# One transformer block for 16 sequences: the feed-forward's chain moved one gap on, its input transposed by VectorE in 32 by 32 blocks, and the head reordered

## The chip, the cores and the metric

The kernel runs on one core of a Trainium2 chip. The metric is the time of one execution on the device in microseconds; of the kernel before there are three timed runs, 646.89, 648.42 and 648.76, and one execution under the profiler, from which every duration below comes.

The engines are called PE (matrix products; its weight loads have a row of their own, PEld), DVE or VectorE, ACT or ScalarE, POOL or GpSimd, and SP (which here only issues transfers). Each works through its own queue in order.

## The reference

Sixteen sequences of 256 tokens with 256 features go through one block, all in float32:

```python
x = x + attention(layernorm(x), wq, wk, wv, wo)    # 16 heads of 16; key j is masked for query i if j - i > 16
x = x + feed_forward(layernorm(x))                 # down(silu(gate(x)) * up(x)), 1024 wide
```

The three weights of the feed-forward are not given as matrices. Each is a cubic spline through 2033 control points, sampled at 262,144 places, and has to be built on the chip.

## The kernel before

**Steps.** The loop over `s` (line 788) runs 20 steps; in the steady part one step works on several sequences at once. `nb = s - 1` has the maxima of its scores found, `tb = s - 2` has its exponentials and values computed, `ob = s - 3` gets its attention output projected and its second norm, sequence `s - 4` goes through the feed-forward, and `pb = s + 3` has q, k and v projected. Scores are computed twice: once for the row maxima (`find_max`, VectorE, tile `z`), once with the maximum as a seventeenth row of k and q for the exponentials (`e`, ScalarE, then a causal cut on POOL).

**Gaps.** PE's four score groups of a step (`inner` 0 and 1, `outer` 0, `inner` 2 and 3, `outer` 1) use the same two PSUM tiles, `scores0` and `scores1`. So a group can only start when VectorE and ScalarE have read the one before it. Between the groups lie numbered gaps, and the order of the work in them is written out by hand: `project(s, gap)` (line 761, with the table `early` for steps 0 to 3, line 721) and `fill(s, gap)` (line 692), which deals out the feed-forward:

- `gate_up(b, i)` (line 588), i = 0 to 3: a quarter of gate and of up (tiles `pg`, `pu`), then tanh on ScalarE (`th`) and two products on VectorE (`th`, `inter`). With `columns=32` each product is issued as four of 32 columns.
- `down(b, c)` (line 609), c = 0 and 1: one half of the tokens, 8 products of PE (`pd`), one add on VectorE into `x`; after c = 1 the sequence's output is sent by SP. Before, `down` could be split again into halves.

Before the change gate_up 0 of a sequence stands in gap 7 of the step in which its second norm is made; gate_up 1, 2 and 3 and down 0 and 1 follow in gaps 1, 3, 4, 5 and 6 of the next step. For steps from 13 on, where nothing is left to project, they stand in gaps 1, 2, 3, and the four half downs in 4, 5, 6 and 6.5.

**The second norm.** In gap 5 `project_o` (line 555, PE tile `py`, needs `divide`) and `stats_f` run, then `norm_f` (line 572, VectorE, tile `xnf`). In gap 6 `turn_f` (line 575) transposes `xnf` into `x2T`, which gate and up read: four PE transposes by the identity into the PSUM tile `ptf`, then a copy by ScalarE.

**The softmax's chain.** `turn_max` (line 486) transposes the maxima (`pm`), copies them (`mxT`) and has SP send them into `qk` in four transfers; the next step's second scores read them. `gather` sends the sums and outputs (`den`, `ac`), `invert` makes reciprocals (`rec`), sends them out and back spread (`rd`, `rb`), and `divide` multiplies before `project_o`. All of it goes through SP's queue.

**The head.** Steps 0 to 3 also load the input, normalise and transpose the first sequences with PE (`stats_a`, `norm_a`, `turn_a`: `xna`, `pta`, `xT`), fill the constant rows of `qk` and `v` with POOL memsets (`scores_and_values`), and build the weights (`spline` through `part`: products `pw`, a ScalarE copy, a predicated VectorE copy). With the home "ssss" the spline's products lie in the two score tiles. `spread(b)` sends q and k of a sequence to `qk` in eight SP transfers.

Nearly every instruction is recorded under line 88, that of the helper that keeps the order; so the profile's groups are told apart by tiles.

Of the kernel before, what the change touches and what calls it, by code (L numbers as in the profile page):

```python
# [11 lines left out]
F32 = mybir.dt.float32  # L12
BF16 = mybir.dt.bfloat16
AF = mybir.ActivationFunctionType
ALU = mybir.AluOpType
# [3 lines left out]
P = 128  # L19
# [74 lines left out]
def block_kernel(  # L94
# [31 lines left out]
    xs = {}  # L126
# [124 lines left out]
    def transposed(src, dst, nm, engine=act):  # L251


        pt = ps_m.tile([P, 2, S], F32, tag="m", name=f"p{nm}")
        for c in range(2):
            for kc in range(2):
                pe.transpose(
                    pt[:, kc, c * P : (c + 1) * P],
                    src[:, c, kc * P : (kc + 1) * P],
                    ident,  # L260
                )
        if engine:
            copied(engine, dst, pt)
        else:
            for kc, engine in enumerate((act, dve)):
                copied(engine, dst[:, kc, :], pt[:, kc, :])
# [184 lines left out]
    def outer(nb, tb, g2):  # L451
        has_n, has_t = 0 <= nb < B, 0 <= tb < B
        qn, qt = qks[nb % NQK], qks[tb % NQK]
        for gi in range(2):
            g, at = 2 * g2 + gi, W0 * gi
            if has_n:
                scores(qn, True, g, 0, at, HB + LOOK)
                scores(qn, True, g, HB, at, P + LOOK)
            if has_t:
                scores(qt, False, g, P, at + HB + LOOK, W1)  # L460
                scores(qt, False, g, P + HB, at + JB, W1 - HB)
        def exponentials(pr):
            e = sb4.tile([P, 2, 2, W1], F32, tag="e1", name=f"e1{tb}_{g2}_{pr}")
            act.activation(
                e,
                tiles[pr][:, :, 0 : 2 * W0].rearrange("p r (g c) -> p r g c", g=2)[
                    :, :, :, W0 - W1 : W0
                ],
                AF.Exp,
                scale=HD**-0.5,  # L470
            )
            pool.affine_select(
                out=e[:, :, :, 0:P], in_=e[:, :, :, 0:P],
                compare_op=ALU.is_ge, fill=0.0, base=I1 + LOOK - P,
                pattern=[[0, 2], [0, 2], [1, P]], channel_multiplier=-1,
            )
            es[tb, 1, g2, pr] = e

        def maxima(pr):
            for r in (2 * pr, 2 * pr + 1):  # L480
                for gi in range(2):
                    find_max(nb, 2 * g2 + gi, r, 0, W0 * gi, JB)

        read(exponentials if has_t else None, maxima if has_n else None)
# [87 lines left out]
    def norm_f(b):  # L572
        x2s[b] = normed(b, "f")

    def turn_f(b):
        x2Ts[b] = sb.tile([P, 2, S], F32, tag="x2T", name=f"x2T{b}")
        transposed(x2s.pop(b), x2Ts[b], f"tf{b}", act if b else None)

    def product(out, lhsT, rhs, start, stop, columns=P):

        for at in range(0, P, columns):
            pe.matmul(
                out[at : at + columns], lhsT=lhsT[:, at : at + columns], rhs=rhs,
                start=start, stop=stop,
            )
# [18 lines left out]
        dve.scalar_tensor_tensor(th, th, 1.0, pp[0], ALU.add, ALU.mult)  # L604
        dve.tensor_tensor(inters[b][:, 2 * i : 2 * i + 2, :], th, pp[1], ALU.mult)

    pds = {}

    def down(b, c, half=None, columns=P):

        inter = inters[b]
        if (b, c) == (B - 1, 1):

            for n in range(0, DIM, P):
                at = slice(n, n + P)
                pd = ps_f.tile([P, P], F32, tag="f", name=f"pd{b}_{c}_{n}")
                for ic in range(8):
                    pe.matmul(
                        pd, lhsT=inter[:, ic, P:], rhs=downT[:, ic, at],
                        start=(ic == 0), stop=(ic == 7),  # L620
                    )
                dve.tensor_tensor(xs[b][:, c, at], xs[b][:, c, at], pd, ALU.add)
                (act if n else sp).dma_start(out[b][P:, at], xs[b][:, c, at])
            return
        if half != 1:
            pds[b, c] = ps_f.tile([P, DIM], F32, tag="f", name=f"pd{b}_{c}")
        for ic in range(8) if half is None else range(4 * half, 4 * half + 4):
            product(
                pds[b, c], inter[:, ic, c * P : (c + 1) * P], downT[:, ic, :], ic == 0, ic == 7,
                columns,  # L630
            )
        if half == 0:
            return
        dve.tensor_tensor(xs[b][:, c, :], xs[b][:, c, :], pds.pop((b, c)), ALU.add)
        to = out[b].rearrange("(c p) d -> p c d", p=P)
        if b == B - 1:
            sp.dma_start(to[:, c, :], xs[b][:, c, :])
        elif c == 1:
            sp.dma_start(to, xs.pop(b))
# [41 lines left out]
    def do(stage, b, *args):  # L681
        if 0 <= b < B:
            stage(b, *args)
# [7 lines left out]

    def fill(s, gap):


        if s < B - AHEAD:
            order = (
                (1, gate_up, 1, 32), (3, gate_up, 2), (4, gate_up, 3, 32), (5, down, 0),
                (6, down, 1),
            )
        else:  # L700
            order = (
                (1, gate_up, 1, 32), (2, gate_up, 2), (3, gate_up, 3), (4, down, 0, 0, 32),
                (5, down, 0, 1), (6, down, 1, 0), (6.5, down, 1, 1),
            )
        for at, stage, *what in order:
            if at == gap:
                if s == B + 3 and stage is down:

                    if what[1] == 0:
                        down(B - 1, what[0])  # L710
                else:
                    do(stage, s - 4, *what)
        if gap == 7:
            do(gate_up, s - 3, 0)

    def part(i, home="ffmm"):
# [9 lines left out]
            (project_part, 1, 0, "f"), (part, 0, "fmmf"),  # L728
        ),
        (1, 1): (  # L730
            (scores_and_values, 2), (turn_a, 2), (project_part, 1, 1), (spread, 1), (stats_a, 3),
        ),
        (1, 2): ((project_part, 2, 0), (coefficients, 1)),
        (1, 3): (
            (project_part, 2, 1), (spread, 2), (norm_a, 3), (scores_and_values, 3),
            (project_v, 1, act, (0,)),
        ),
        (1, 4): ((project_v, 1, act, (1,)), (turn_a, 3), (stats_a, 4)),
        (1, 5): ((part, 1),),
        (1, 6): ((scores_and_values, 4), (project_qk, 3)),  # L740
        (1, 7): (
            (spread, 3), (stats_a, 5), (part, 2, "ssss"), (norm_a, 4), (project_v, 2),
        ),
        (2, 1): ((turn_a, 4), (norm_a, 5), (scores_and_values, 5)),
        (2, 2): ((project_part, 4, 0), (turn_a, 5), (coefficients, 2), (stats_a, 6)),
        (2, 3): ((project_part, 4, 1), (spread, 4), (project_part, 5, 0)),
        (2, 4): ((norm_a, 6), (project_v, 3, act, (0,))),
        (2, 5): ((project_part, 5, 1), (spread, 5)),
        (2, 6): ((project_v, 3, act, (1,)), (project_v, 4)),
        (2, 7): ((part, 3, "ssss"), (part, 4)),  # L750
        (3, 1): ((turn_a, 6),),
        (3, 2): ((project_part, 6, 0), (sum_weights, "q"), (center, "q")),
        (3, 3): (
            (project_part, 6, 1), (spread, 6), (sum_weights, "k"), (sum_weights, "v"),
            (center, "k"), (center, "v"),
        ),
        (3, 6): ((project_v, 6), (project_v, 5)),
        (3, 7): ((part, 5, "ssss"),),
    }

    def project(s, gap):
# [26 lines left out]
    for s in range(B + 4):  # L788
        nb, tb, ob = s - 1, s - 2, s - 3

        pairs = s == B + 1
        inner(nb, tb, *((0, 1) if pairs else (0,)))
        if ob < B - 1:
            do(values, ob, 1)
            do(gather, ob)
        project(s, 1)
        fill(s, 1)
        if not pairs:
            inner(nb, tb, 1)
        do(invert, ob)  # L800
        if s:
            do(load_x, s + 2 + AHEAD)
        project(s, 2)
        fill(s, 2)
        outer(nb, tb, 0)
        project(s, 3)
        fill(s, 3)
        if pairs:
            do(values, tb, 0)
            inner(nb, tb, 2, 3)  # L810
        else:
            inner(nb, tb, 2)
            do(values, tb, 0)
        project(s, 4)
        do(divide, ob)
        fill(s, 4)
        if not pairs:
            inner(nb, tb, 3)
        do(project_o, ob)
        do(stats_f, ob)  # L820
        project(s, 5)
        fill(s, 5)
        if s != 3:
            do(norm_f, ob)
        outer(nb, tb, 1)
        fill(s, 6)
        if s == 3:

            project(s, 6)
            norm_f(ob)  # L830
            turn_max(nb)
        do(turn_f, ob)
        if s != 3:
            project(s, 6)
        fill(s, 6.5)
        if tb == B - 1:
            values(tb, 1)
            gather(tb)
        if s != 3:
            do(turn_max, nb)  # L840
        project(s, 7)
        fill(s, 7)

# [29 lines left out]
```

## Time and profile before

| | |
|---|---|
| median of three runs | 648.42 us |
| the profiled execution | 651.59 us |
| its span, first to last instruction | 649.4 us |
| mean granted clock of PE | 0.995 |
| PE busy | 638.7 us, 98% |
| VectorE busy | 369.6 us, 57% |
| ScalarE busy | 215.0 us, 33% |
| POOL busy | 130.6 us, 20% |
| one step of the steady part (326.65 to 364.75) | 38.10 us, VectorE busy 22.16 |
| PE transposes `ptf` | 64 records, 9.7 us busy |
| ScalarE copies `x2T` from `ptf` | 15 of 584 ns and one in two parts |

How to read it: a row of the timeline gives the start in us from the span's start, the duration, the engine, the line, the operation, the tiles (output, arrow, inputs), the shape and the number of instructions merged; in brackets, the idle time before it and what ended it. Each float32 product of PE appears as two records. Matmuls overlap, so the time that a run of them takes is read from its start to the start of the next run. `PEclk` is the share of PE's full clock that was granted.

### The profile page before, as it was taken

What the parts mean: (1) busy time and instruction counts of PE and PEld (TensorE: products, weight loads), DVE (VectorE), ACT (ScalarE), POOL (GpSimd) and SP (SyncE); (2) the same over time, 40 slices, a digit from 0 to 9 for tenths busy, and PEclk for the clock granted to TensorE, in tenths of its full rate; (3) what the DMA queues carried; (4) which work ended last, traced back from release to release, by engine and by line L of the source; (5) the groups of instructions that cost most, each with busy time, mean ns of one, the idle gap of its engine ahead of it and who ended that gap; (6) DMA issues with size and microseconds to landing.
All of it is one profiled execution on the core that took longest, in us unless ns stands there. A gap on an engine that the chain in (4) does not pass through costs nothing.

```text
span 649.4 us, 21145 instructions
## 1 busy us (share of the span) xinstructions
PE 638.7 (98%) x8740; PEld 476.5 (73%) x8740; DVE 369.6 (57%) x1487; ACT 215.0 (33%) x382; POOL 130.6 (20%) x255
## 2 busy tenths in 40 slices
PE   8989999999999999999999999999999999999998
PEld 7566667777778777787877778777777777777777
DVE  6875566646465664646566464655656564733342
ACT  1355343233332323333232332323333333333110
POOL 4342222211121211112112121211212030212000
PEclk9999799999999999999999999999999999999999
DMA  5733141414132131323214131210010101010100
GB/s 177 173 67 58 33 85 33 75 37 86 34 73 46 38 75 36 86 36 73 46 31 81 36 71 33 55 33 21 19 36 21 36 21 31 24 36 19 52 17 17
DMA packets 40767, 33.36 MB, mean 51 GB/s; under 512 B 10592, under 2 KB 40032, under 8 KB 40672
## 3 DMA queue, kind: packets, MB, share of 16 engines
q1 hardware_dynamic: 39392, 30.90, 21.5%
q8 instruction: 69, 1.13, 0.8%
q10 hardware_dynamic: 1280, 1.11, 0.6%
q14 instruction: 26, 0.21, 0.3%
HBM read 14.42 MB, written 4.47 MB: 29 GB/s over the span
## 4 chain that ended last, share of the span: by engine, by line
PE 95%; DVE 2%; POOL 1%; issue 1%; ACT 1%; DMA 0%; another core or an unknown queue 0%; POOLq 0%; ACTq 0%; DVEq 0%
PE pg L88 18%; PE pd L88 18%; PE pu L88 17%; PE scores L88 16%; PE po L88 7%; PE py L88 5%; PE pq L88 5%; PE pk L88 4%; PE pv L88 3%; PE ptf L88 1%; DVE z L88 1%; PE pm L88 1%; PE pta L88 0%; ACT e L88 0%; PE pw L88 0%
## 5 line engine op out<-in xcount | busy, mean ns | idle before, releaser
L88 ACT ACTIVATE e<-scores 128x512 f32<-128x512 f32 (+1 forms) x192 | 117.2, 615 | 270.9 <-PE scores L88 219.6
L88 DVE CUSTOM_DVE_ANT_0 z<-scores,mask 128x144 bf16<-128x144 f32 (+1 forms) x512 | 154.5, 362 | 52.7 <-PE scores L88 34.5
L88 POOL TENSOR_SCALAR_AFFINE_SELECT e<-e 128x224 f32<-128x224 f32 (+1 forms) x192 | 94.5, 493 | 405.5 <-ACT e L88 402.3
L88 PE MATMUL pg<-x2T,gateT 128*32 128x256 f32 (+1 forms) x1112 | 123.9, 381 | 0.0
L88 PE MATMUL pu<-x2T,upT 128*32 128x256 f32 (+1 forms) x1112 | 121.4, 379 | 0.0
L88 PE MATMUL pd<-downT,inter 128*128 128x256 f32 (+2 forms) x672 | 119.1, 377 | 0.0
L88 PE MATMUL scores<-qk 17*64 17x144 f32 (+7 forms) x4096 | 107.4, 319 | 4.2 <-ACT e L88 1.5
L88 DVE SCALAR_TENSOR_TENSOR th<-th,pg 128x512 f32<-128x512 f32 x64 | 44.0, 688 | 114.5 <-ACT th L88 114.5
L88 PEld LDWEIGHTS pd<-downT,inter 128*128 128x128 f32 (+1 forms) x672 | 93.2, 167 | 15.8 <-DVE ac L88 0.4
L88 PEld LDWEIGHTS pu<-x2T,upT 128*32 128x32 f32 (+1 forms) x1112 | 85.3, 133 | 25.2
L88 PEld LDWEIGHTS scores<-qk 17*64 17x64 f32 (+1 forms) x4096 | 70.0, 132 | 41.5 <-issue 29.8
L88 PEld LDWEIGHTS pg<-x2T,gateT 128*32 128x32 f32 (+1 forms) x1112 | 82.0, 132 | 25.2 <-DVE th L88 1.9
L88 ACT ACTIVATE th<-pg 128x512 f32<-128x512 f32 x64 | 38.2, 597 | 66.9 <-PE pg L88 66.3
L88 DVE TENSOR_TENSOR inter<-th,pu 128x512 f32<-128x512 f32 x64 | 44.0, 687 | 26.3 <-PE pu L88 26.3
L88 PE MATMUL po<-e,v 128*32 128x256 f32 (+1 forms) x1024 | 51.3, 342 | 0.0
L88 PEld LDWEIGHTS po<-e,v 128*32 128x32 f32 x1024 | 30.0, 111 | 24.2 <-issue 13.5
L88 DVE DVE_READ_ACCUMULATOR2_ANT mx<- 128x1 f32 x512 | 42.3, 83 | 0.0
L88 DVE TENSOR_TENSOR x<-x,pd 128x256 f32<-128x256 f32 (+1 forms) x33 | 13.6, 411 | 41.8 <-PE pd L88 41.8
L88 PE MATMUL pq<-xT,wq 128*128 128x256 f32 x128 | 31.7, 391 | 0.5 <-ACT xT L88 0.5
L88 PE MATMUL py<-wo,ac 128*128 128x256 f32 x128 | 31.9, 392 | 0.0
L88 PE MATMUL pk<-xT,wk 128*128 128x256 f32 x128 | 30.8, 383 | 0.2 <-DVE gateT L88 0.2
L88 PEld LDWEIGHTS py<-wo,ac 128*128 128x128 f32 x128 | 23.0, 189 | 8.7 <-DVE inter L88 3.5
(81 smaller groups left out, 385.4 us busy)
## 6 DMA issues: line engine op xcount, KB each, us to landing
qk<-qkc SPq DMA_DIRECT2D x124, 64.0 KB
x<-x SPq DMA_DIRECT2D x16, 256.0 KB
ac<-au SPq DMA_DIRECT2D x128, 32.0 KB
rb<-rd SPq DMA_DIRECT2D x32, 128.0 KB
out<-x SPq DMA_DIRECT2D x15, 256.0 KB
xT<-xT SPq DMA_DIRECT2D x9, 256.0 KB
fa<-ra SPq DMA_DIRECT2D x9, 128.0 KB
qk<-mxT SPq DMA_DIRECT2D x64, 4.0 KB
```

Source lines behind the costliest of these rows:

```text
L88: return self.tc.keep_in_program_order(fn(*args, **kwargs))
```

## The change

Five things change.

1. `turn_f`: for all sequences but the last, VectorE transposes `xnf` straight into `x2T`, by sixteen instructions of 32 partitions by 128 elements, each of which turns four blocks of 32 by 32. There is no PSUM tile and no ScalarE copy. The last sequence keeps PE and ScalarE's copy.
2. In the loop `turn_f` stands ahead of the feed-forward's part of gap 6 (behind it for the last sequence). In step 3, `norm_f` and `turn_f` come behind `turn_max`.
3. `fill`: the chain stands one gap later. gate_up 0 to 3 and down 0 and 1 now lie in gaps 1, 3, 4, 5, 6 and 7 of the step after the norm; from step 13 on in gaps 1, 2, 3, 4, 6 and 7, and gap 5 has none. gate_up 0 and 2 (from step 13 on 0 and 3) have the 32-column form.
4. `down` is no longer split into halves and has no 32-column form.
5. `early`: the memsets of the sequences 2 to 5 come later (behind `stats_a` of the sequence or the next gap), `stats_a(4)`, the halves of `project_v(3)` and `project_v(5)` and the scores' fillers move, and `spread(5)` moves from gap 5 of step 2 to gap 7, behind `turn_max`.

In instructions: PE loses 60 transposes, ScalarE 15 copies, and VectorE gets 240 transposes and loses one copy. The products of gate and up in 32-column form grow from 400 to 512 each; 96 such of `pd` go, and 24 full ones take their place.

```diff
     def turn_f(b):
         x2Ts[b] = sb.tile([P, 2, S], F32, tag="x2T", name=f"x2T{b}")
-        transposed(x2s.pop(b), x2Ts[b], f"tf{b}", act if b else None)
+        if b == B - 1:
+            transposed(x2s.pop(b), x2Ts[b], f"tf{b}")
+            return
+        src = x2s.pop(b).rearrange("p c (kc d) -> p c kc d", kc=2)
+        dst = x2Ts[b].rearrange("p kc (c t) -> p c kc t", c=2)
+        for m in range(0, P, 32):
+            for q in range(0, P, 32):
+                dve.transpose(
+                    dst[m : m + 32, :, :, q : q + 32], src[q : q + 32, :, :, m : m + 32]
+                )
...
         if s < B - AHEAD:
             order = (
-                (1, gate_up, 1, 32), (3, gate_up, 2), (4, gate_up, 3, 32), (5, down, 0),
-                (6, down, 1),
+                (1, gate_up, 0, 32), (3, gate_up, 1), (4, gate_up, 2, 32), (5, gate_up, 3),
+                (6, down, 0), (7, down, 1),
             )
         else:
             order = (
-                (1, gate_up, 1, 32), (2, gate_up, 2), (3, gate_up, 3), (4, down, 0, 0, 32),
-                (5, down, 0, 1), (6, down, 1, 0), (6.5, down, 1, 1),
+                (1, gate_up, 0, 32), (2, gate_up, 1), (3, gate_up, 2), (4, gate_up, 3, 32),
+                (6, down, 0), (7, down, 1),
             )
...
-        if gap == 7:
-            do(gate_up, s - 3, 0)
...
         (1, 1): (
-            (scores_and_values, 2), (turn_a, 2), (project_part, 1, 1), (spread, 1), (stats_a, 3),
+            (turn_a, 2), (project_part, 1, 1), (spread, 1), (stats_a, 3), (scores_and_values, 2),
         ),
...
-            (project_part, 2, 1), (spread, 2), (norm_a, 3), (scores_and_values, 3),
-            (project_v, 1, act, (0,)),
+            (project_part, 2, 1), (spread, 2), (norm_a, 3), (project_v, 1, act, (0,)),
         ),
-        (1, 4): ((project_v, 1, act, (1,)), (turn_a, 3), (stats_a, 4)),
+        (1, 4): ((project_v, 1, act, (1,)), (turn_a, 3), (scores_and_values, 3)),
         (1, 5): ((part, 1),),
-        (1, 6): ((scores_and_values, 4), (project_qk, 3)),
+        (1, 6): ((project_qk, 3),),
         (1, 7): (
-            (spread, 3), (stats_a, 5), (part, 2, "ssss"), (norm_a, 4), (project_v, 2),
+            (spread, 3), (stats_a, 4), (stats_a, 5), (part, 2, "ssss"), (norm_a, 4),
+            (project_v, 2), (scores_and_values, 4),
         ),
-        (2, 1): ((turn_a, 4), (norm_a, 5), (scores_and_values, 5)),
+        (2, 1): ((turn_a, 4), (norm_a, 5), (project_v, 3, act, (0,))),
...
-        (2, 4): ((norm_a, 6), (project_v, 3, act, (0,))),
-        (2, 5): ((project_part, 5, 1), (spread, 5)),
+        (2, 4): ((norm_a, 6),),
+        (2, 5): ((project_part, 5, 1),),
         (2, 6): ((project_v, 3, act, (1,)), (project_v, 4)),
-        (2, 7): ((part, 3, "ssss"), (part, 4)),
+        (2, 7): ((spread, 5), (part, 3, "ssss"), (part, 4)),
...
-        (3, 6): ((project_v, 6), (project_v, 5)),
-        (3, 7): ((part, 5, "ssss"),),
+        (3, 6): ((project_v, 6), (project_v, 5, act, (0,))),
+        (3, 7): ((part, 5, "ssss"), (project_v, 5, act, (1,))),
...
         outer(nb, tb, 1)
+        if 0 < ob < B - 1:
+            turn_f(ob)
         fill(s, 6)
-        if s == 3:
-            project(s, 6)
-            norm_f(ob)
-            turn_max(nb)
-        do(turn_f, ob)
-        if s != 3:
-            project(s, 6)
-        fill(s, 6.5)
+        if ob == B - 1:
+            turn_f(ob)
+        project(s, 6)
...
-        if s != 3:
-            do(turn_max, nb)
+        do(turn_max, nb)
+        if s == 3:
+            norm_f(ob)
+            turn_f(ob)
         project(s, 7)
         fill(s, 7)
```

More of the change, by code (lines that the diff above doesn't have):

```diff
@@ L605, in gate_up, with down @@
         dve.tensor_tensor(inters[b][:, 2 * i : 2 * i + 2, :], th, pp[1], ALU.mult)
-    pds = {}
-    def down(b, c, half=None, columns=P):
+    def down(b, c):
         inter = inters[b]
@@ L624, in down @@
             return
[L625 to L630, printed above, removed]
-            )
-        if half == 0:
-            return
-        dve.tensor_tensor(xs[b][:, c, :], xs[b][:, c, :], pds.pop((b, c)), ALU.add)
+        pd = ps_f.tile([P, DIM], F32, tag="f", name=f"pd{b}_{c}")
+        for ic in range(8):
+            pe.matmul(
+                pd, lhsT=inter[:, ic, c * P : (c + 1) * P], rhs=downT[:, ic, :],
+                start=(ic == 0), stop=(ic == 7),
+            )
+        dve.tensor_tensor(xs[b][:, c, :], xs[b][:, c, :], pd, ALU.add)
         to = out[b].rearrange("(c p) d -> p c d", p=P)
@@ L706, in fill @@
             if at == gap:
[L707 to L712, printed above, removed]
-        if gap == 7:
-            do(gate_up, s - 3, 0)
+                do(stage, s - 4, *what)
     def part(i, home="ffmm"):
@@ L734, in block_kernel @@
         (1, 3): (
-            (project_part, 2, 1), (spread, 2), (norm_a, 3), (scores_and_values, 3),
-            (project_v, 1, act, (0,)),
+            (project_part, 2, 1), (spread, 2), (norm_a, 3), (project_v, 1, act, (0,)),
         ),
-        (1, 4): ((project_v, 1, act, (1,)), (turn_a, 3), (stats_a, 4)),
+        (1, 4): ((project_v, 1, act, (1,)), (turn_a, 3), (scores_and_values, 3)),
         (1, 5): ((part, 1),),
-        (1, 6): ((scores_and_values, 4), (project_qk, 3)),
+        (1, 6): ((project_qk, 3),),
         (1, 7): (
-            (spread, 3), (stats_a, 5), (part, 2, "ssss"), (norm_a, 4), (project_v, 2),
-        ),
-        (2, 1): ((turn_a, 4), (norm_a, 5), (scores_and_values, 5)),
-        (2, 2): ((project_part, 4, 0), (turn_a, 5), (coefficients, 2), (stats_a, 6)),
+            (spread, 3), (stats_a, 4), (stats_a, 5), (part, 2, "ssss"), (norm_a, 4),
+            (project_v, 2), (scores_and_values, 4),
+        ),
+        (2, 1): ((turn_a, 4), (norm_a, 5), (project_v, 3, act, (0,))),
+        (2, 2): (
+            (project_part, 4, 0), (turn_a, 5), (coefficients, 2), (stats_a, 6),
+            (scores_and_values, 5),
+        ),
         (2, 3): ((project_part, 4, 1), (spread, 4), (project_part, 5, 0)),
-        (2, 4): ((norm_a, 6), (project_v, 3, act, (0,))),
-        (2, 5): ((project_part, 5, 1), (spread, 5)),
+        (2, 4): ((norm_a, 6),),
+        (2, 5): ((project_part, 5, 1),),
         (2, 6): ((project_v, 3, act, (1,)), (project_v, 4)),
-        (2, 7): ((part, 3, "ssss"), (part, 4)),
+        (2, 7): ((spread, 5), (part, 3, "ssss"), (part, 4)),
         (3, 1): ((turn_a, 6),),
```

## The prediction

> **What bounds the kernel now.** I read the page's head first: which engine is full, and whether its clock is.
>
> ```profile
> PE 638.7 (98%) x8740; PEld 476.5 (73%) x8740; DVE 369.6 (57%) x1487; ACT 215.0 (33%) x382; POOL 130.6 (20%) x255
> ...
> PEclk9999799999999999999999999999999999999999
> ...
> PE 95%; DVE 2%; POOL 1%; issue 1%; ACT 1%; DMA 0%; another core or an unknown queue 0%; POOLq 0%; ACTq 0%; DVEq 0%
> ```
>
> PE is busy 98% of the span and is 95% of the chain of waits; VectorE has 43% free. One slice, the fifth, has a lower clock. A mean hides stages, so next the table by stretch:
>
> ```profile
> 62.00:76.00 14.00, 12.29 (x128) 6.71 (x126) 7.20 (x27) 6.26 (x12) 1.88 (x5) 0.76 0.26 41
> ...
> 98.50:639.00 540.50, 540.45 (x7638) 405.96 (x7638) 301.48 (x1196) 174.51 (x306) 98.17 (x191) 1.00 0.20 43
> ```
>
> The second column is the stretch's length, then PE's busy time; the 1.00 is the clock. From 98.5 to 639 us PE has no hole: 540.45 of 540.50. There only taking work off PE helps. The head (to 98.5) has holes and a stretch at a clock of 0.76: there order decides. So the two halves are priced apart.
>
> **The loop: what leaves PE.** PE's timeline around one turn_f, in the step from 288.6 to 326.6:
>
> ```profile
> 317.59 3.72 PE L88 MATMUL pd<-downT,inter 128*128 128x256 f32 x16
> 321.15 0.60 PE L88 MATMUL ptf<-ident,xnf 128*128 128x128 f32 x4
> 321.58 1.89 PE L88 MATMUL pv<-wv,xT 128*128 128x256 f32 x8
> ```
>
> Matmuls overlap, so a run costs start to start: the transposes ptf take 321.58 - 321.15 = 0.44 us. The change takes them off PE for batches 0 to 14. Batches 1 to 14 lie in the gapless part: 14 x 0.44 = **6.2 us**. (Batch 0 is in the head's sum; batch 15 stays on PE.)
>
> The other PE work only moves. Gap 5 has gate_up 3 for a down half (1.73 + 1.82 = 3.55 against 3.55), gap 7 down 1 for gate_up 0 (3.55 each), gap 1 gate_up 0 for gate_up 1, both in 32-column form. From step 13 on, gaps 4 to 7 hold 1.84 + 1.83 + 1.82 + 1.83 + 0.44 + 1.73 + 0.22 + 1.73 + 1.82 = 13.26 before (from 490.5 us on, without scores and values); after, gate_up 3 (3.57), project_o with its change of tiling (1.92), down 0 (3.56), pm (0.22), down 1 (3.55): 12.82, again 0.44 less. There gap 5 keeps project_o alone as cover between two score groups. The second exponential of the group before ends at 312.86, 1.72 us after its scores (311.14): 0.2 us of cover is left, and each tenth beyond it would cost five tenths in all.
>
> **The loop: what VectorE gets.** Sixteen transposes of 32 x 128 elements a batch, 240 in all, of a kind that this trace does not have. The nearest rows are VectorE's own: back to back, instructions of 256 elements start 0.34 us apart and of 512 0.61, so about 0.07 + n/960; for 128 elements 0.205 us, or **3.3 us a batch**. The floor is zero. The far row is the reciprocal: 64 elements, 0.465 us to the next, or 0.86 to 0.93 for 128 and 15 us a batch. I take 0.205, since many kinds share that slope, and keep both ends.
>
> What hides it: VectorE's timeline in the same place.
>
> ```profile
> 321.35 0.42 DVE L88 TENSOR_TENSOR x<-x,pd 128x256 f32<-128x256 f32 x1 [1.50 <-PE pd L88]
> 326.09 0.69 DVE L88 SCALAR_TENSOR_TENSOR th<-th,pg 128x512 f32<-128x512 f32 x1 [4.32 <-ACT th L88]
> ```
>
> VectorE idles 1.50 and 4.32 us here, after maxima that end at 319.83. After the change norm_f waits behind gate_up 3's two products, so they end some 0.25 later, near 320.1. Behind the transposes stand down 0's add (0.42) and the next maxima. PE needs x2T, and the bank that down 0's add frees, at gate_up 0: 317.59 + 3.56 (down 0) + 1.73 (pv) + 0.22 (pm) + 3.55 (down 1) + 0.97 (scores) + 1.38 (values) = 329.0. So a transpose may take (329.0 - 320.1 - 0.42)/16 = **0.53 us** before PE waits; at 0.205 the cover is over twice the need, and they cost nothing. ScalarE loses a copy of 0.58, off the path. The output's transfer is issued some 5.5 us later (after the add at 326.9 instead of 321.35), behind turn_max's transfers in SP's queue, not ahead of them; the next thing behind it, a gather, needs the values' copy near 329.6. It delays nobody.
>
> [...]
>
> **The head.** Reading the timeline by step, four edits matter.
>
> (a) Memsets. norm_a(2) on VectorE, whose halves are 0.41 us elsewhere:
>
> ```profile
> 16.97 0.95 POOL L88 MEMSET qk<- 128x1024 f32 x1
> ...
> 17.06 2.21 DVE L88 TENSOR_SCALAR xna<-x,mva,rstda 128x256 f32<-128x256 f32 x2 [0.81 <-POOL rstda L88]
> ```
>
> It lasts 2.21 instead of 0.73, as long as POOL's memsets, which run to 19.05: 1.5 us in a step whose scores wait for VectorE's maxima (each group starts within 0.1 of the last maximum). Behind stats_a(3) these memsets meet no tensor_scalar; those for batches 3 and 4 now may meet norm_a(3) and norm_a(4) for some 0.5 each, which I set against the smaller gains of (b). Gain **1.5**.
>
> (b) stats_a(4) leaves the maxima's queue, and project_v(3)'s half covers a hole of 1.2 us in step 2, gap 1, but leaves gap 4 0.3 short: net **0.5** of a sum of 1.5, the rest lost to (a)'s new meetings.
>
> (c) SP's queue. The eight transfers of spread(5), 0.64 us each, stand ahead of turn_max's in step 2:
>
> ```profile
> 62.28 0.41 DVE L88 COPY mxT<-pm 16x256 f32<-16x256 f32 x1 [0.88 <-PE pm L88]
> ...
> 65.21 2.26 SPq L88 DMA_DIRECT2D qk<-mxT  x4
> ...
> 67.02 1.82 PE L88 MATMUL scores<-qk 17*64 17x208 f32 x24 [1.10 <-DMA qk<-mxT]
> ```
>
> The maxima are ready at 62.70, their transfer goes at 65.21, and PE waits to 67.02, though its tiles are free from 65.35: 1.7 us. Then the clock halves (0.50 from 66.8 to 73.6 in the stretches): scores, values, a transpose and scores take 74.05 - 67.02 = 7.03 where they take 0.8 + 1.49 + 0.55 + 1.0 = 3.84 at full clock: 3.2. Together **4.9** to gain. Against it: spread(5) now delays gather(0). From the first maxima transfer it is 2.3 + 8 x 0.64 + 2.3 + 2.6 (den, ac) + 0.5 + 2.6 (rd, ac) + 0.7 to the last rb issue, 3.1 more to its landing (585.51 to 588.5 in the one step where divide waits), 0.7 for divide: 19.9, or 17.9 from the first scores, where PE's work to project_o needs 15.8 (20.7 less 4.9). **2** go back.
>
> (d) Step 3's end loses gate_up 0 as cover, and VectorE transposes batch 0 there, ahead of the downT predicated copies that free the score tiles. From the end of the outer scores: maxima +3.0, norm_f 0.73, transposes 3.3, copies 0.6 and 0.7: tiles at 7.6 and 8.3. PE has pv 2.69, pm 0.22, pw 0.96, pv 0.96 = 4.8, then waits. Before, this stood at 6.46 (88.45 to 94.91), the 0.44 of ptf included. **1.6** go back; with free transposes it would be a gain of 1.7, at the reciprocal's rate a loss of some 13.
>
> Head: 1.5 + 0.5 + 4.9 - 2 - 1.6 = 3.3 us. **Sum: 6.2 + 3.3 = 9.5 us.** The profiled execution took 651.59 us (span 649.4 and 2.2 around it): 642.1. It lay 3.2 above the median of the three runs (648.42), so for the median: 648.4 - 9.5 = **638.9**.
>
> **Rivals.**
> 1. *The head gives its part back.* The clock halved after a window in which PE mostly waited; (d) makes a wait of about 3 us after light work. If it halves there, up to 3.4 us (half of 6.8) go, and with SP's chain a little longer nothing is left of 3.3: 648.4 - 6.2 = 642.2, to 645 if more is lost. For it: two new waits. Against it: all else in the loop shows a clock of 1.00.
> 2. *The head keeps more.* (c)'s return and (d) come out small: 6.2 + 6 to 7, or 636.
> 3. *Slower: VectorE's transposes become the bound.* From 0.53 us each PE waits at gate_up 0 in every step; from (9.5/14)/16 = 0.04 more, 0.57, the kernel is slower than before. At 0.93: 16 x 0.93 = 14.9, so 320.1 + 14.9 + 0.42 - 329.0 = 6.4 a step, 14 x 6.4 = 90 and 13 in the head: about 740. For it: no row of this kind. Against it: every streaming row lies on the 0.205 line.
> 4. *Moved, not removed:* a wait in steps 13 to 17 (gap 5's thin cover) and in each step's new order eats the 6.2: 648. PE's slack in the rows says no.
>
> **How the numbers follow.** Forecast (637 to 641.5) 0.60; head given back 0.23; more kept 0.09; no change 0.04; slower 0.04. About 0.3% is what a measurement of this kernel can tell from no change. Faster: 0.60 + 0.23 + 0.09 = 0.92; same 0.04; slower 0.04. The range takes the forecast and both neighbours: 635 to 645; left out are the last two cases and the edges.
>
> **What would show it.** In the loop: no ptf on PE, step length 38.10 (326.65 to 364.75) down to 37.66, transposes 0.2 us apart and ended before 324. In the head: mxT's transfer directly behind its copy, scores of step 3 without a DMA wait, clock 1.00 there; then a wait of project_o for divide and of step 4's scores for downT. I am wrong if steps stay at 38.1, if transposes start over 0.5 apart, or if a new stretch at half clock stands near step 4.

## The result and the profile after

The changed kernel takes 656.19 us (median of six runs, 654.6 to 656.79), the kernel before 648.59 beside it (646.89 to 650.0): ratio 1.0099, 95% interval 1.0071 to 1.0127. In a second comparison (e12_after_again) it was 656.98 against 651.12, ratio 1.0088 (1.0063 to 1.0113). It is slower by 1%; I had forecast 1.5% faster. The profiled execution took 655.93, its span is 654.2, 4.8 more than before. The medians differ by 7.6: the profiled execution of the kernel before lay 3 us above its median, so some 2.8 us of the loss are not in the two traces.

The page's head of the changed kernel, line for line as before:

```profile
PE 634.2 (97%) x8872; PEld 467.7 (71%) x8872; DVE 440.1 (67%) x1726; ACT 206.6 (32%) x367; POOL 130.5 (20%) x255
...
PEclk9999988999999999999999999999999999999999
...
PE 81%; DVE 6%; SPq 2%; issue 1%; DMA 1%; POOL 1%; DVEq 0%
```

PE is busy 4.5 us less, and yet the span is longer. On the chain of waits PE fell from 95% to 81%; VectorE and SP's queue took the place. Two slices at a lower clock stand where before was one. The table by stretch says where (columns as before: the stretch's length, then PE, PEld, VectorE, ScalarE and POOL busy, the clock, DMA):

```profile
62.00:76.00 14.00, 12.47 (x196) 8.74 (x192) 9.54 (x45) 6.83 (x13) 3.01 (x7) 1.00 0.32 52
76.00:104.00 28.00, 20.56 (x290) 12.76 (x294) 18.45 (x76) 8.82 (x18) 5.37 (x11) 0.82 0.28 59
137.73:175.38 37.65, 37.65 (x548) 28.29 (x547) 26.82 (x107) 11.86 (x21) 7.33 (x14) 1.00 0.28 56
438.90:472.66 33.76, 32.64 (x524) 23.65 (x523) 23.23 (x96) 11.15 (x19) 6.60 (x13) 1.00 0.10 27
```

The third line is a step of the loop: 37.65 us with no hole, 0.44 less than before, as forecast. The first two are the head: the stretch from 62 to 76 has its clock back (1.00 for 0.76), but from 76 to 104 PE stands 7.4 of 28 us and the clock is 0.82. The last is step 13: 33.76 us with a hole of 1.1; the same step took 32.91 before. The timeline of the changed kernel shows three waits that were not there. First, in the head, VectorE's reciprocal and then PE's project_o:

```profile
72.98 0.55 DVE L88 RECIPROCAL rec<-den 64x64 f32<-64x64 f32 x1 [3.93 <-DMA den<-au]
...
81.71 0.69 DVE L88 TENSOR_TENSOR ac<-ac,rb 128x512 f32<-128x512 f32 x1 [2.85 <-DMA x<-x]
82.50 3.58 PE L88 MATMUL py<-wo,ac 128*128 128x256 f32 x8 [2.45 <-DVE ac L88]
```

PE waits 2.45 us for divide (the row `ac<-ac,rb`), and py then runs at half clock: 3.5 us to the next run instead of 1.9. The row puts divide's own wait down to the load of x, which divide doesn't read; it reads rb, and the experiment that moves spread(5) alone (e2) ends the wait. Then step 3's end:

```profile
91.12 5.05 DVE L88 STREAM_TRANSPOSE x2T<-xnf 32x128 f32<-32x128 f32 x16
92.00 1.07 ACT L88 COPY downT<-scores 128x512 f32<-128x512 f32 x2 [0.71 <-PE scores L88]
96.20 1.32 DVE L88 COPY_PREDICATED downT<-second_in,scores 128x512 f32<-128x512 uint8 x2
96.98 2.44 PE L88 MATMUL scores<-qk 16*64 16x208 f32 x32 [3.95 <-DVE downT L88]
```

The sixteen transposes take 5.05 us, 0.316 from start to start; the predicated copies, whose input ScalarE has ready at 93, stand behind them, and PE waits 3.95 us for the tiles. Its clock is then half for 6.83 us. Third, in steps 13 to 16:

```profile
465.99 1.03 DVE L88 TENSOR_SCALAR xnf<-x,mvf,rstdf 128x256 f32<-128x256 f32 x2 [0.81 <-POOL rstdf L88]
466.93 0.30 DVE L88 CUSTOM_DVE_ANT_0 z<-scores,mask 128x144 bf16<-128x144 f32 x1
...
468.89 0.39 PE L88 MATMUL pm<-ident,mx 128*16 128x128 f32 x2 [1.12 <-DVE mx L88]
```

norm_f waits for POOL's rstdf, the outer maxima stand behind norm_f, and pm waits for the last maximum. Before, PE had 8.71 us of work from project_o to pm in these steps (494.67 to 503.38 in step 14), with one half down ahead of the outer scores, two more and ptf behind them; now it has project_o, the outer scores and down 0, 6.72 us (461.05 to 467.76).

**Account of the 4.8 us**, from the starts of project_o in the two traces. There the changed kernel has done less of the feed-forward than the kernel before, one gate_up in steps 4 to 12 (3.55 us) and half a down from step 13 on (1.83), which is counted as still to do: the head +5.1, steps 4 to 12 nine times -0.44 = -4.0, steps 13 to 16 four times (33.76 - 32.91) = +3.4, the rest +0.3.

### The profile page after: what moved, and what is told of

It is laid out like the page before. It is cut to its first block, busy times and chain, and to the rows that moved or that the text cites. A ratio compares the mean times of both kernels' runs of the same rounds, so it can differ in the third digit from the quotient of the medians.

```text
span 654.2 us, 21635 instructions
## 1 busy us (share of the span) xinstructions
PE 634.2 (97%) x8872; PEld 467.7 (71%) x8872; DVE 440.1 (67%) x1726; ACT 206.6 (32%) x367; POOL 130.5 (20%) x255
## 4 chain that ended last, share of the span: by engine, by line
PE 81%; DVE 6%; SPq 2%; issue 1%; DMA 1%; POOL 1%; DVEq 0%
PE pg L88 18%; PE pu L88 17%; PE pd L88 14%; PE scores L88 12%; PE po L88 7%; PE py L88 5%; PE pv L88 3%; PE pk L88 3%; PE pq L88 3%; SPq L88 2%; DVE x2T L88 1%; DVE z L88 1%; DVE x L88 1%; DVE statsf L88 1%; DVE xnf L88 1%
## 5 line engine op out<-in xcount | busy, mean ns | idle before, releaser
L88 PE MATMUL pd<-downT,inter 128*128 128x256 f32 (+1 forms) x528 | 117.4, 376 | 0.0
L88 PEld LDWEIGHTS pd<-downT,inter 128*128 128x128 f32 x528 | 95.5, 190 | 13.6 <-issue 0.4
L88 PEld LDWEIGHTS pu<-x2T,upT 128*32 128x32 f32 (+1 forms) x1280 | 81.8, 126 | 28.7
L88 PEld LDWEIGHTS pg<-x2T,gateT 128*32 128x32 f32 (+1 forms) x1280 | 79.6, 126 | 28.9 <-DVE th L88 1.9
L88 DVE STREAM_TRANSPOSE x2T<-xnf 32x128 f32<-32x128 f32 x240 | 72.6, 302 | 3.1
L88 PE MATMUL py<-wo,ac 128*128 128x256 f32 x128 | 33.5, 407 | 2.5 <-DVE ac L88 2.5
```

Source lines behind the costliest of these rows:

```text
L88: return self.tc.keep_in_program_order(fn(*args, **kwargs))
```

## The experiments

Three theories were set against each other. **Q**: three waits in VectorE's and SP's queues cost the time, and each goes when one operation is moved. **T**: VectorE's transposes weigh on the whole loop. **C**: it is the half clock in the head, whatever the waits. Each run is compared with the kernel before on its own chip.

| run | median us | ratio to before (95%) |
|---|---|---|
| after (first, again) | 656.19, 656.98 | 1.0099 (1.0071-1.0127), 1.0088 (1.0063-1.0113) |
| e1_norm_late | 651.97 | 1.0019 (0.9986-1.0052) |
| e2_spread_late | 653.57 | 1.0032 (1.0002-1.0062) |
| e3_first_on_pe | 652.40 | 0.9996 (0.9962-1.0031) |
| e4_all_three | 646.23 | 0.9927 (0.9904-0.9951) |
| e5_spread6_behind | 643.68 | 0.9892 (0.9862-0.9921) |
| e6_all_on_pe | 651.14 | 1.0009 (0.9987-1.0032) |
| e7_before_vector | 729.72 | 1.1201 (1.1156-1.1245) |
| e8_twice | 699.76 | 1.0746 (1.0708-1.0785) |
| e9_xT_behind | 641.06 | 0.9853 (0.9829-0.9877) |
| e10_xT_early | 643.99 | 0.9904 (0.9866-0.9942) |
| e11_thirty_five | 718.31 | 1.1035 (1.1005-1.1065) |

**e1_norm_late.** From step 13 on, norm_f behind the outer score group's maxima:

```diff
-        if s != 3:
+        late = s == 3 or s >= B - AHEAD
+        if not late:
             do(norm_f, ob)
         outer(nb, tb, 1)
+        if s != 3 and late:
+            do(norm_f, ob)
```

> The changed kernel, with norm_f behind the outer score group instead of ahead of it in the steps from 13 on; all else as it is. Theory Q (queues: the loss is made by three waits, one of them turn_max's for the maxima that stand behind norm_f in VectorE's queue in steps 13 to 16, 1.29 us each): the wait goes, PE's steps 13 to 16 fall from 33.76 to 32.5, the time by 4 x 1.29 = 5.2 us against the changed kernel's 656.2, to about 651. Rival T (transposes: the sixteen transposes of 0.316 us a batch weigh on VectorE in every step, and the waits are only where this shows): the maxima come earlier but the work is the same, so the wait turns up elsewhere in the same steps, and the time stays within 1 us of 656. Rival C (clock: what was lost is the half clock in the head alone): no effect either, 656.

Steps 13 to 15 fall from 33.76 to 32.47 (project_o at 461.32, 493.79, 526.25, 558.72), and pm follows down 0 directly:

```profile
464.32 3.72 PE L88 MATMUL pd<-downT,inter 128*128 128x256 f32 x16
...
467.88 0.38 PE L88 MATMUL pm<-ident,mx 128*16 128x128 f32 x2
```

That is 1.29 a step, 5.2 in four, and 0.44 below the kernel before: the third wait is settled. By the ratios the kernel is 4.5 to 5.2 us faster than the changed kernel (1.0019 against 1.0088 and 1.0099), where T and C gave no change. The head of this profile lost more to the clock than after's (10.2 us at half from 82.3).

**e2_spread_late.** spread(5) in gap 2 of step 3, behind the chain's last transfers, instead of ahead of gather(0):

```diff
-        (2, 7): ((spread, 5), (part, 3, "ssss"), (part, 4)),
+        (2, 7): ((part, 3, "ssss"), (part, 4)),
-        (3, 2): ((project_part, 6, 0), ...
+        (3, 2): ((spread, 5), (project_part, 6, 0), ...
```

> The changed kernel, with spread(5)'s eight transfers moved once more, from gap 7 of step 2 to gap 2 of step 3, behind gather's and invert's transfers. Theory Q: the sums of sequence 0 reach VectorE some 3 us earlier, divide no longer waits, project_o starts right after its scores (2.5 us of wait gone) and at full clock (1.6 us more): 4 us less, about 652. The later wait for downT stays as it is. Rival T: no transpose is touched, 656. Rival C: the time gained is only kept if the clock does not halve at another place; the second stretch at half clock (6.8 us near step 4) may move or grow, so 653 to 657.

divide is in time and project_o runs at full clock:

```profile
77.48 0.69 DVE L88 TENSOR_TENSOR ac<-ac,rb 128x512 f32<-128x512 f32 x1 [0.32 <-DMA x<-x]
78.28 1.99 PE L88 MATMUL py<-wo,ac 128*128 128x256 f32 x8
```

project_o starts 4.2 us earlier than in after (82.50), and the next score group 5.8 earlier. The hole at step 3's end and its half clock (6.83 us) remain, neither longer nor shorter. By the ratios it is 3.6 to 4.4 us faster than the changed kernel, as Q said; the median, 653.57, lies in C's range too, and only the trace tells them apart.

**e3_first_on_pe.** Sequence 0, whose norm lies at step 3's end, is transposed by PE again:

```diff
-        if b == B - 1:
-            transposed(x2s.pop(b), x2Ts[b], f"tf{b}")
+        if b in (0, B - 1):
+            transposed(x2s.pop(b), x2Ts[b], f"tf{b}", act if b else None)
```

> The changed kernel, with the transposes of sequence 0 alone back on PE (four transposes, the copy split over ScalarE and VectorE, as in the kernel before); the fourteen others stay on VectorE. Theory Q: the downT copies no longer stand behind 5 us of transposes; PE's hole before step 4's first scores (4.1 us) shrinks to about 1, and the half clock that follows it (3.1 us lost) goes: 5 to 6 us less, about 650.5. Rival T: one batch of fifteen is freed, 1/15 of the loss, under 1 us: 655.5. Rival C: if the first wait, that for divide, is enough to halve the clock at step 4 too, only the hole goes: 653.

The hole of 3.95 us at 93 is gone; step 4's scores start at 96.58 after a wait of 0.37. But after the wait for divide the clock stayed half for 10.24 us instead of 3.41, up to 92:

```profile
82.84 3.75 PE L88 MATMUL py<-wo,ac 128*128 128x256 f32 x8 [2.76 <-DVE ac L88]
```

So the single effect of e3 can't be read from its profile to better than a few us. Seven of its ten runs had a higher granted clock (0.995 or 0.997) than this one (0.992). By the ratios it is 6.0 to 6.7 us faster than the changed kernel, near Q's 5 to 6; T had under 1.

**e4_all_three.** The three edits together.

> The changed kernel with all three edits: norm_f late from step 13 on, spread(5) in gap 2 of step 3, sequence 0 transposed by PE. Theory Q: the three waits are apart in time, so the effects add: 656.2 - 5.2 - 4 - 5.5 = 641.5, some 1.1% below the kernel before (648.6), and the clock is 1.00 all along. Rival T: still about 655. Rival C: like Q if no half clock is left, else 645 to 650.

646.23 us, faster than before by 0.7%. Q had 14.7 us less than the changed kernel; by the ratios it is some 11, 4 short. The rest is a fourth wait, 2.06 us with 3.41 at half clock behind it, which the other three had hidden:

```profile
85.15 0.36 ACT L88 COPY mxT<-pm 16x256 f32<-16x256 f32 x1 [0.20 <-PE pm L88]
...
89.22 2.30 SPq L88 DMA_DIRECT2D qk<-mxT  x4
91.52 1.47 PE L88 MATMUL scores<-qk 17*64 17x208 f32 x24 [2.06 <-DMA qk<-mxT]
```

mxT is ready at 85.51, but its transfer is issued 3.7 us later: spread(5), moved, pushed spread(6) and the load of xT(7) to where turn_max's transfers should go.

**e5_spread6_behind.** e4 with spread(6) behind turn_max as well:

```diff
-            (project_part, 6, 1), (spread, 6), (sum_weights, "k"), (sum_weights, "v"),
+            (project_part, 6, 1), (sum_weights, "k"), (sum_weights, "v"),
-        (3, 7): ((part, 5, "ssss"), ...
+        (3, 7): ((spread, 6), (part, 5, "ssss"), ...
```

> The three edits together (e4_all_three) and one more: the eight transfers of spread(6) go from gap 3 of step 3 to gap 7, behind turn_max, so that they no longer stand ahead of the maxima's transfers in SP's queue. Theory Q (waits in VectorE's and SP's queues): the mxT transfers go at about 86 instead of 89.22, the scores of step 4's first group lose their 2.06 us wait for DMA and most of the half clock behind it (about 1.5 of PE's time): 3 to 4 us less than e4_all_three, 642.5 to 643.5. Theory T (VectorE's transposes weigh on the whole loop): they are untouched, and the head is too small a part: within 1 us of e4_all_three. Theory C (the clock of the head decides): about 1.7 us less, only if the half clock goes.

The median is near Q's number, but its interval overlaps e4's, and the profile shows no gain in this place: the transfers were issued at once, and PE waited as before.

```profile
86.05 2.32 SPq L88 DMA_DIRECT2D qk<-mxT  x4
...
92.34 1.39 PE L88 MATMUL scores<-qk 17*64 17x208 f32 x24 [2.36 <-DMA qk<-mxT]
```

Issued 3.2 us earlier than in e4, they let PE go at 92.34, there at 91.52. So the issue is not all of a transfer's wait; e9 and e10 ask what the rest is.

**e6_all_on_pe.** e5 with every sequence on PE, behind down 0; VectorE transposes nothing:

```diff
-        if b in (0, B - 1):
+        if b < B:
...
-        if 0 < ob < B - 1:
-            turn_f(ob)
         fill(s, 6)
-        if ob == B - 1:
+        if 0 < ob < B:
             turn_f(ob)
```

> As e5_spread6_behind, but every sequence is transposed by PE with ScalarE's copy, behind down 0 in gap 6; VectorE has no transposes. Theory Q: in the loop they were hidden, so PE gets back 0.44 us for each of 14 sequences: 6 us slower than e5_spread6_behind, near 649. Theory T: 240 transposes go, 72.6 us of VectorE, and the kernel becomes faster than e5_spread6_behind by several us.

651.14 against 643.68: 7.5 us slower (5.4 in the spans). T is refuted: taking 67 us of work off VectorE costs time, since PE is the full engine (98% busy in e5). A step is 38.09 again; steps 13 to 15 take 33.24 instead of 32.47.

**e7_before_vector.** The kernel before, with VectorE transposing sequences 1 to 14 and nothing else changed (chain and head as before; `turn_f` as in the change, but for sequences 0 and 15).

> The kernel before with one part of the change alone: VectorE transposes sequences 1 to 14 where PE did, the chain stays where it was (gate_up 0 in gap 7 of the same step). Theory Q: VectorE can start at about 321.8 (behind down 1's add) and needs 5.05, to 326.9, while PE has work until 323.3 (down 1, project_v, pm): about 3.6 us of wait less the 0.44 saved, some 3.2 a step and 14 steps, 45 us slower: near 693. With the 0.205 us each of the prediction it would be 1.4 a step and near 668. Theory T: the same loss as in the changed kernel, 5 to 10 us.

79 us slower than before, nearly twice what Q gave (45). A step takes 44.37 instead of 38.09:

```profile
348.21 5.04 DVE L88 STREAM_TRANSPOSE x2T<-xnf 32x128 f32<-32x128 f32 x16
...
353.30 3.78 PE L88 MATMUL pg<-x2T,gateT 128*128 128x256 f32 x8 [3.52 <-DVE x2T L88]
```

The wait is what Q gave (3.52 for some 3.6). What I had left out is the clock behind it, in the table by stretch:

```profile
353.30:359.88 6.58, 6.58 (x17) 5.05 (x17) 0.69 (x1) 0.60 (x1) 0.00 (x0) 0.55 0.14 22
```

Here gate_up 0 takes 6.6 us instead of 3.6 at a clock of 0.55. It takes 6.4 to 6.6 in nine of the thirteen steps with such a wait, 5.2 to 5.3 in the other four. So the transposes alone are a heavy loss, and the chain's move by a gap is what makes them free.

**e8_twice.** e5 with each of VectorE's transposes issued twice.

```diff
-                dve.transpose(
+                for _ in range(2):
+                    dve.transpose(
...
```

> As e5_spread6_behind, but each of VectorE's transposes is issued twice (work doubled, result the same). Theory Q: thirty-two take 10.1 us, from 274.4 to 284.5 in one step of the loop, and down 0's add stands behind them, to 284.95; PE needs the bank and x2T at 283.7: 1.3 to 1.5 us of wait in each of 9 steps, about 2 in the 5 with the late norm: some 23 us slower than e5_spread6_behind, 655 to 672. Theory T: every transpose costs its own time, 14 x 5.05 = 71 us slower, over 705.

In steps 4 to 12 it went as Q said: 5.4 us more of VectorE cost PE a hole of 1.3 to 1.5 us (3.05 in one step), at full clock.

```profile
282.84 10.43 DVE L88 STREAM_TRANSPOSE x2T<-xnf 32x128 f32<-32x128 f32 x32
...
293.78 0.42 PE L88 MATMUL pg<-x2T,gateT 128*32 128x256 f32 x4 [1.47 <-DVE x L88]
```

A step is 39.32 against 37.65. In steps 13 to 16 Q was far too low: a hole of 5.1 instead of about 2 (project_v's 1.73 is missing from the cover, and norm_f comes later), and a half clock of 3.4 or 6.8 us behind it: 39.1 to 40.6 for steps 13 to 15 where e1 has 32.47. Nine times 1.67, 30 in steps 13 to 16 and 7.8 in step 17 are 52.8, which is the difference of the spans; the medians differ by 56.

**e9_xT_behind and e10_xT_early.** e5 with the load of xT(7), 256 KB, behind turn_max (e9), or ahead of spread(5), long before it (e10):

```diff
-        (3, 7): ((spread, 6), ...
+        (3, 7): ((load_xT, 7), (spread, 6), ...
-            if at == gap and b >= RAW:
+            if at == gap and b >= RAW and (stage, b) != (load_xT, RAW):
```

> As e5_spread6_behind, where the maxima's transfers were issued 3.2 us earlier than in e4_all_three (86.05 against 89.22) and yet the scores of step 4 waited until 92.34. Here the load of xT(7), 256 KB, goes behind turn_max as well, so that nothing issued after 81.5 stands ahead of the maxima's transfers. Theory F (the transfers queue in the DMA engines behind xT, which in e5_spread6_behind landed in part only by 92.0): mxT lands near 88.5, the scores run at 88.9 without a wait and the half clock behind it goes: 4.84 + 2.64 become 1.0 + 1.4 in PE's rows, 5 us less: 638 to 640. Theory S (DMA packets are slow from 86.5 to 90.5 whatever the order; many took 0.9 to 2 us there): mxT still lands after 91, no gain.

> As e5_spread6_behind, but the load of xT(7) goes ahead of spread(5), at about 76.3, and is done long before turn_max. Theory F: the same as e9_xT_behind, mxT lands near 88.5: 638 to 640. Theory S: mxT still lands after 91, as e5_spread6_behind, 643 to 645.

In both the scores of step 4 no longer wait for the maxima: F holds, S falls. The times alone would not say so: e9 is 1 us above F's range, and e10 lies in S's. In e9 the first and the second scores run as one row of 32 (in e5 the wait stands behind the first 8):

```profile
86.25 2.64 SPq L88 DMA_DIRECT2D qk<-mxT  x4
89.00 0.38 SPq L88 DMA_DIRECT2D xT<-xT  x1
89.02 1.63 PE L88 MATMUL scores<-qk 16*64 16x208 f32 x32 [0.37 <-DVE downT L88]
```

From 76 to 104 e9's PE is busy 26.04 of 28 us at a clock of 1.00, and from there on nothing is at half clock but the last 1 us. It is the fastest version by its median, 0.9853 of before (its interval overlaps e10's). In e10 the 256 KB meet another chain: rb is issued at 73.6 and 74.3, as in e4, and the load at 75.5, behind it; yet divide comes at 78.96 where e4 has 77.48, PE waits 1.38 us, and py is at half clock. Of the three places tried, only behind turn_max does nobody wait for the load. Which of its packets held up which transfer was not measured. With the load at e5's place the wait for the maxima was 2.36, 1.73, 0.52 and 2.03 us in four traces (e5, e6, e8, e11); the two other places were traced once each.

**e11_thirty_five.** e8 with three transposes more (`for _ in range(2 + (m == 0 and q > 0))`), for a wait between e8's and e7's.

> As e8_twice, with three transposes more in a batch: 35 for 16, 0.95 us more, so that PE's wait in a step of the loop grows from 1.65 to 2.6 us. If it is the length of a wait that halves the clock afterwards, somewhere between 1.65 (no half clock in e8_twice's steps 4 to 12) and 3.7 (half clock in every step of e7_before_vector): either the steps grow by 0.95 to 40.3 (no half clock; the whole 13 us over e8_twice, 713), or by 0.95 and the 3 us of a 6.8 us stretch at half clock, to 43.3 (740).

Between the two answers: the holes are 2.5 us (2.2 to 2.8), and behind six of the nine the clock is half for 3.41 us, behind the others not.

```profile
261.36:264.15 2.79, 0.01 (x2) 0.01 (x1) 2.61 (x9) 0.00 (x0) 0.00 (x0) 1.00 0.02 3
264.64:268.05 3.41, 3.41 (x40) 1.69 (x36) 2.35 (x14) 1.67 (x3) 1.07 (x2) 0.50 0.24 81
303.69:306.20 2.51, 0.04 (x4) 0.04 (x6) 2.35 (x8) 0.00 (x0) 0.00 (x0) 1.00 0.03 7
306.20:313.00 6.80, 6.80 (x107) 4.54 (x108) 6.12 (x26) 2.77 (x5) 1.83 (x4) 1.00 0.21 61
```

**e12_after_again.** The changed kernel, unaltered.

> The changed kernel itself, unaltered, beside the other three on the same chip: about 656, 1.007 to 1.013 of the kernel before. Its profile shows whether the waits at 82.5 (divide), 92 to 97 (downT behind the transposes) and in steps 13 to 16 (pm) stand again, with the half clock behind the first two.

All three waits stand again, with half clock at 83.3 (3.41 us) and at 97.0 (6.83 us).

## Why the prediction was wrong, step by step

Three steps failed: the cover in steps 13 to 16 (5.2 us off), what (c) gives back (3.4 off) and (d) (4.9 off). The move itself, transposing on VectorE in the loop, did what was forecast in steps 4 to 12.

**The loop, steps 4 to 12: right.** 37.65 for 38.09; ptf's 0.44 is saved and PE has no hole.

**The transposes' price: mis-sized.** "I take 0.205, since many kinds share that slope": it is 0.316. The slope came from instructions whose ends overlap the next one's start (0.42 long, 0.34 apart); transposes are 0.302 long and start 14 ns after the last one's end. In steps 4 to 12 this costs nothing: the changed kernel's transposes stay inside the cover of 0.53 each.

```profile
281.37 5.04 DVE L88 STREAM_TRANSPOSE x2T<-xnf 32x128 f32<-32x128 f32 x16
...
286.45 0.42 DVE L88 TENSOR_TENSOR x<-x,pd 128x256 f32<-128x256 f32 x1
```

The cover was sized well: e8, at 0.65 for each of the sixteen places, has a wait of 1.5 us, which puts it at 0.56. In (d) the price counts in full.

**Steps 13 to 16: failed.** For "There gap 5 keeps project_o alone as cover" I followed the second exponential, which frees a tile, and found 0.2 us. The order in VectorE's queue was not followed: norm_f, with its wait for POOL, stands ahead of the outer maxima, and turn_max's pm needs the last of them; with 6.72 us of PE's work for 8.71 ahead of pm, the last maximum comes 1.12 us too late. Rival 4 named just this place, and I set it aside with "PE's slack in the rows says no": +0.85 a step instead of -0.44. e1 takes the wait away and gets the -0.44.

**(a) and (b): right together.** Step 3's first scores come at 62.62 for 64.75: 2.1 for 2.0. The two were not measured apart.

**(c): gain right, return failed.** The halved stretch and the DMA wait went; up to step 3's third score group that is 4.7 for 4.9. Of the 4.9, 3.2 were the half clock of one execution (6.83 us of it, a mean clock of 0.995). Of the 63 runs of the kernel before beside the experiments, 32 had a mean clock of 0.997 or more, by which under 5 us were at half (an estimate: 649 us x 0.0035 / 0.5 = 4.5); so half of the executions had less of this to gain than the sum took off. But I let 2 go back, and it was 5.4. My sum followed SP's chain to divide, and that wait is 2.45. Not in it were the reciprocal, which waits 3.93 us for den in VectorE's queue with `center` and the maxima behind it (1.35 us of PE between 72.9 and 76.1), and py at half clock (1.6). e2, which moves spread(5) only, removes all three.

**(d): right mechanism, far too small.** 3.4 instead of 1.6 (its own rows give 1.2 for the first tile and 1.9 for the second), the difference being the transposes (16 x 0.11 = 1.8); then the half clock on scores, po and pg: 3.1 more. Rival 1 had the price (3.4 us) and the place of this halving, and got 0.23; it happened twice. It rested on a misreading, that the clock before had halved after a window in which PE "mostly waited": from 62.00 to 66.70 PE was busy 3.31 of 4.70 us. The sign of being wrong that came true was the last one named, a new stretch at half clock near step 4.

So the head: -2.1 - 4.7 + 5.4 + 6.5 = +5.1 instead of -3.3; the loop -0.3 instead of -6.2. That no case but the 0.04 of rival 3 lay above 648 was the wider fault: every new wait was priced alone, at full clock, and none behind an in-order queue. That the total of e9 (0.9853) is about what the sum promised the change is luck: e9 has five edits that the change has not.

## What to carry to other kernels

Where an instruction that waits is put ahead of others in an in-order queue, price everybody who waits for those behind it: here norm_f ahead of the maxima, the reciprocal ahead of `center`, the transposes ahead of the predicated copies, spread ahead of gather. A transfer issued early need not land early: in e5 the maxima's transfers were issued at once, with a load of 256 KB ahead of them, and PE waited 2.36 us; with the load behind them (e9) it did not wait for them. So issue the load behind the urgent transfer, and look whom it meets there (in e10, with the load just behind rb, divide came 1.48 us later than in e4). On PE a new hole is to be priced with the half clock that may stand behind it: in the changed kernel this cost 1.6 us behind 2.45 and 3.1 behind 3.95, and in e11 six of nine holes of 2.2 to 2.8 us had one. And a stretch at half clock in one trace is not in every execution.

## What the runs showed of the hardware

PE's clock behind a hole in its work, over e7, e8 and e11: behind eight holes of 1.3 to 1.5 us and one of 3.05 in steps 4 to 12, and one of 1.71 in step 17, no half clock; behind holes of 2.2 to 2.8, in six of nine; behind 3.5 us and more, in all 23 cases, for 3.41 or 6.83 us. In the head half clock stood behind holes of 1.10 us (before), 1.38 us (e10) and 1.73 us (e6).

The hole's length alone does not sort these cases: two holes of e11 of nearly the same length ended differently, the one at 344.01 (2.48 us) with half clock behind it, the one at 303.69 (2.47) without. What sorts them was not shown. In the two traces of the changed kernel the first half clock starts at different times, 82.37 and 83.32 (e12).

VectorE's transposes of 32 x 128 float32 take 302 ns and start 316 ns apart (sixteen in 5.04 us at 281.37), where its maxima of 256 elements (0.42 us) start 0.34 apart in the same trace (99.58 to 100.96) and two adds of 256 take 0.75 (e8, 293.30): these overlap, the transposes do not.
